# A masked dense layer and a LoRA layer on one core: the first loads cut in halves, fewer products with zeros, later loads of the first batch whole

## The chip, the cores and the metric

The kernel runs on one core of a Trainium2 chip. The metric is the time of one execution on the device in microseconds; lower is better. All data are fp32, and a mask is int32. Before the change the median of three runs is 395.52 us (395.45 to 395.57).

## The reference, cut to what matters

Eight batches of 256 tokens with 1024 features go through two linear layers, each with a residual. The first layer adds to its weight W0 a sign matrix, made from a mask of the batch's own and scaled by a coefficient of the batch. The second adds a product of rank 16 to a shared weight W1.

```python
# first layer: x is (8, 256, 1024), W (1024, 1024), mask (8, 1024, 1024)
output = einsum('bsi,oi->bso', x, W0) + b0
sign = 2 * mask - 1
x = x + output + einsum('bsi,bio->bso', x, sign) * coeff[:, None, None]
# second layer
base = einsum('bti,oi->bto', x, W1) + b1
lora = einsum('btr,bro->bto', einsum('bti,bir->btr', x, A[slot]), B[slot])
x = x + base + lora * 2.0
```

## The kernel before, in words

**One weight for each batch.** For batch b the kernel builds `coeff*(2*mask - 1) + W0 (+ identity, for the residual)` in SBUF and multiplies it with the batch's tokens. ScalarE turns the mask into the scaled sign (`convert`, L483 to L493, its records on L488); VectorE adds W0 (`add`, L385, records on L387); TensorE multiplies.

**Batch 0 is dense.** Its weight has 1024 input rows, cut into eight chunks c of 128 rows; a chunk has two parts i of 512 output columns. Loads of mask and W0 for each part (256 KB each, 2048 bytes to a partition) are issued on SP's queue in the order mask, W0, part after part (L522 to L531). The tokens of batch 0 come in between: chunk 0's on ACT's queue, chunk 1's on SP's (128 KB each), and those of two chunks at a time behind the first part of chunks 2, 4 and 6 (256 KB each). W0 stays in SBUF; later batches load masks only. For chunk 0, `parts` (L462) cuts the first part into two halves of 256 columns for converting, adding and multiplying, while the loads bring the part whole. The 64 matmuls of the dense batch (L570) run chunk after chunk, each 128x128 weights by 256 tokens. Each fp32 matmul shows as two passes in the records, so they are 128.

**Ahead of it** TensorE runs products with zeros (`idle`, L419, records on L422), which compute nothing that is used: columns 256 and 128 first, then one small product that spreads the coefficients over the partitions (L435), then 256, 256 and 128 columns (L441). From the coefficients VectorE makes `two_c` and `neg_c` (L445), which every convert needs.

**Batches 1 to 7** use products by quarter blocks with sums of weights and of tokens (`seven`, L718, seven products in place of eight; TensorE records on L761). Batch 1's masks go another way (L645). Masks come in blocks of 512 KB, 4096 bytes to a partition. **The second layer** works on four batches at a time with the same scheme twice over, and partly three times (`Deep`, records on L1144; plain leaves on L1089). Leaves of W1 that the second group of batches needs again are written to DRAM by the first group and loaded again (`left_again`, L919). Where a name is in `HALVES`, the saved innermost sums come as two loads of 128 KB in place of one of 256 KB (L943).

**The order of the work** is planned ahead of the run. `Plan.task` notes each piece of work with the time it should take; `plan.pe` is the time at which TensorE is expected to be free, from which due times come; `plan.order` (L153) then places all pieces on the five engines by a greedy rule, with a model of DMA rate and eight DMAs in flight, and picks the buffers. The instructions are issued in that order. First loads have a rank of their own (L517) and so keep the order in which they are written.

Of the kernel before, what the change touches and what calls it, by code (L numbers as in the profile page):

```python
# [9 lines left out]
I32 = mybir.dt.int32  # L10
# [3 lines left out]
P = 128  # L14
OH = 512
CG = 2
OQ = 256
# [6 lines left out]
A22_AT = 40.0  # L24
INNER_MOVED, INNER_AT = ({}, {o: ("t1", "t2", "t3", "t4") for o in ("S3", "A22")}), 24.0
SAVED = {(o, n) for o in ("A11", "S1", "S4") for n in ("a11", "s1")}
HALVES = ("A11",)
EARLIEST = 35.0
SHIFTED, MASKED = 5.2, 1.8
LEAF, SLACK = 30.0, 1.5  # L30
ALONE = 8.0
# [273 lines left out]
def kernel(  # L305
# [17 lines left out]
    NG, _, _, T = x0T.shape  # L323
    R = lora_b.shape[1]
    SLOTS = lora_b.shape[0]
    D = lora_b.shape[2]
# [12 lines left out]
    def fixed(name, shape, dtype=F32):  # L339
        return Buf(name, None, t=const.tile(shape, dtype, tag=name, name=name))  # L340
# [6 lines left out]
    w0_sb = fixed("w0", [P, NC, D])  # L347
# [11 lines left out]
    def big(name, a, b):  # L359
        return Buf(name, "B", (a, b))  # L360
# [4 lines left out]
    def small(name, a, b):  # L365
        return Buf(name, "S", (a, b))
# [12 lines left out]
    plan = Plan(2.9)  # L379
# [14 lines left out]
    def dma(engine, o, x, nbytes, due=None, ahead=None, slack=0.0):  # L394
        busy = {"SP": 0.37, "ACT": 0.36, "POOL": 0.53}[engine]
        reads = [x] if isinstance(x, Ref) else []
        writes = [o] if isinstance(o, Ref) else []

        def emit():
            ENGINE[engine].dma_start(  # L400
                o.ap() if isinstance(o, Ref) else o, x.ap() if isinstance(x, Ref) else x
            )

        return plan.task(
            engine, busy, plan.LATENCY[engine] + slack, emit, reads, writes, due, ahead, nbytes
        )

    def pe(n, busy, emit, reads, writes):
        return plan.task("PE", busy, 0.17, emit, reads, writes)
# [9 lines left out]
    def idle(*columns):  # L419
        def emit():  # L420
            for n in columns:
                nc.tensor.matmul(  # L422
                    idle_ps.t[:, 0, :n], lhsT=zeros[:, :P], rhs=zeros[:, :n], start=True, stop=True
                )

        pe(1, sum(columns) / 290, emit, (), (idle_ps((0,)),))
# [11 lines left out]
        (h_sb(h_rows), lb_pad((0, 1))),  # L438
        (c_ps((0,)),),
    )  # L440
    idle(T, T, T // 2)  # L441
    plan.pe = 5.2
    for o, f in ((two_c, 2.0), (neg_c, -1.0)):
        dve(
            lambda o=o, f=f: nc.vector.tensor_scalar_mul(o.t, c_ps.t[:, 0, :B], f),  # L445
# [6 lines left out]
    def x0_ref(p, c=None):  # L452
        return x0[p](ALL if c is None else (c,), (lambda t: t) if c is None else (lambda t: t[:, c]))
# [4 lines left out]
    def part(a, i):  # L458
        flat = a.rearrange("p i f -> (p i f)")
        return flat.rearrange("(i p f) -> i p f", i=2, p=P)[i]  # L460

    def parts(c):  # L462
        every = slice(0, OH)
        if c == 0:
            return [(0, slice(0, OQ)), (0, slice(OQ, OH)), (1, every)]
        return [(0, every), (1, every)]

    def halves(o):
        return tuple(q for q in range(2) if o.start < (q + 1) * OQ and o.stop > q * OQ)
# [36 lines left out]
    w_b0 = [big(f"w_0_{c}", 2, OH) for c in range(NC)]  # L506

    def w_part(c, i, o):
        return w_b0[c](tuple((i, q) for q in halves(o)), lambda t: t[:, i, o])

    def w0_part(c, i, o):
        return w0_sb(
            tuple((c, i, q) for q in halves(o)),
            lambda t: t[:, c, :].rearrange("p (h o) -> p h o", h=2)[:, i, o],
        )

    def first_loads(*load):  # L517
        k = dma(*load)
        k.rank = 1.0 + 0.001 * k.n

    every = slice(0, OH)
    for c in range(NC):  # L522
        for i in range(2):
            w = w_part(c, i, every)
            m = w.buf(w.keys, lambda t, f=w.index: f(t).bitcast(I32))
            first_loads("SP", m, part(mask[0, c], i), P * OH * 4)
            first_loads("SP", w0_part(c, i, every), part(w0T[c], i), P * OH * 4)
            if c < CG and i == 0:
                first_loads(("ACT", "SP")[c], x0_ref(0, c), part(x0T[0], c), P * T * 4)
            elif c % CG == 0 and i == 0:  # L530
                first_loads("SP", x0_ref(c // CG), x0T[c // CG], P * CG * T * 4)  # L531
# [19 lines left out]
    for c in range(NC):  # L551
        h, q = divmod(c * P, OH)
        for i, o in parts(c):
            w = w_part(c, i, o)
            m = w.buf(w.keys, lambda t, f=w.index: f(t).bitcast(I32))
            n = o.stop - o.start
            convert(w, m, 0, n)
            if c >= 1 and i == h and o.start <= q < o.stop:
                d = w_b0[c](((h, q // OQ),), lambda t, h=h, q=q: t[:, h, q : q + P])
                add(d, d, ident((0,)), P)  # L560
            add(w, w, w0_part(c, i, o), n)
    for c in range(NC):
        for i, o in parts(c):
            ots = [i * TPH + j for j in range(o.start // P, o.stop // P)]
            w = w_part(c, i, o)

            def emit(c=c, ots=ots):
                for ot in ots:
                    h, j = divmod(ot, TPH)
                    nc.tensor.matmul(  # L570
                        dense[ot // 2].t[:, ot % 2, :],
                        lhsT=w_b0[c].t[:, h, j * P : (j + 1) * P],
                        rhs=x0[c // CG].t[:, c % CG, :],
                        start=c == 0 and ot % 2 == 0,
                        stop=c == NC - 1,
                        skip_group_check=True,
                    )

            pe(
                len(ots),  # L580
                len(ots) * 0.4318,
                emit,
                (w, x0_ref(c // CG, c % CG)),
                [dense[d]((0,)) for d in sorted({ot // 2 for ot in ots})],
            )
# [277 lines left out]

    SOON = EARLIEST
    A_OF = {"a11": (0, 0), "a12": (0, 1), "a22": (1, 1)}
# [53 lines left out]
    def left_again(name, pairs=()):  # L919
# [21 lines left out]
        for n in saved:  # L941
            t = small(f"ls_{name}_{n}", 4, P)
            step = 2 if name in HALVES else 4  # L943
            for i in range(0, 4, step):
# [100 lines left out]
    def second_layer(group, before):  # L1045
# [35 lines left out]
        def product(ps, l, r, start=False, part=None):  # L1081
            parts = [(c, j) for c in range(CG) for j in range(2)]
            if part is not None:
                parts = parts[part : part + 1]

            def emit():
                lt, rt = l.ap(), r.ap()
                for c, j in parts:
                    nc.tensor.matmul(  # L1089
                        ps.t[:, j, :],  # L1090
                        lhsT=lt[:, c, j * P : (j + 1) * P],
                        rhs=rt[:, c, :],
                        start=start and c == 0 and j == 0,
                        stop=False,
                        skip_group_check=True,
                    )

            pe(len(parts), len(parts) * 0.4318, emit, (l, r), (ps((0,)),))
# [577 lines left out]
```

## Time and profile before

| | us |
|---|---|
| median of three runs | 395.52 |
| the profiled execution | 395.16 |
| its span, first to last instruction | 393.46 |
| first product with zeros starts | 0.90 |
| first matmul of the dense batch starts | 5.46 |
| first matmul of batch 1 starts | 34.54 |
| DMA: 102.50 MB, mean | 261 GB/s |

The span is what the profile shows of one execution; the execution's own time is longer by what lies around it. PE is TensorE's matmuls, PEld its weight loads, DVE VectorE, ACT ScalarE, POOL GpSimd, SP the engine that issues most DMAs. A row of the timeline gives start, duration, engine, line of the kernel, operation, output and inputs, how many instructions are merged in it, and in brackets how long the engine idled before and what ended that. A row of the chain gives start, duration and what ran. A row by stretches gives the stretch, its length, the busy time of each engine with its instructions, the granted TensorE clock, the DMA engines' share and GB/s.

### The profile page before, as it was taken

To read this page: it belongs to the slowest core of one execution; us is meant where nothing else is said; L and a number is where in the kernel's file an instruction comes from. 1 tells how busy PE (TensorE), PEld (TensorE's weight loads), DVE (VectorE), ACT (ScalarE), POOL (GpSimd) and SP (SyncE) were. 2 spreads that over 40 slices of the span, in tenths; PEclk is the share of its full clock that TensorE was granted. 3 is DMA by queue.
4 is the path that set the end of the run, shared out by engine and by line. 5 is a ranking of instruction groups with operands and counts; after the bars stand their busy time and mean duration, and the time that the engine had idled before them with its cause. 6 is when DMAs were issued, how large, how long until landed. Compare 5 with 4: busy or idle time off the path is not lost.

```text
span 393.5 us, 7725 instructions
## 1 busy us (share of the span) xinstructions
PE 389.7 (99%) x2920; PEld 363.8 (92%) x2920; DVE 352.2 (90%) x596; ACT 169.8 (43%) x314; POOL 84.2 (21%) x140
## 2 busy tenths in 40 slices
PE   9999999999999999999999999999999999999997
PEld 7889999999978898988899999999999789999896
DVE  3569999999897799989999989999996999999886
ACT  5469677516245221315615647373222563431210
POOL 1000202234734264252250330000000131241000
PEclk9999999999999999999999999999999999999999
DMA  8999999994899969989999998503702999995804
GB/s 290 389 389 410 404 300 389 318 346 156 198 269 290 270 239 368 417 247 317 348 347 338 291 260 304 191 1 108 242 0 61 262 238 265 324 255 101 263 31 185
DMA packets 39382, 102.50 MB, mean 261 GB/s; under 512 B 5170, under 2 KB 6322, under 8 KB 39346
## 3 DMA queue, kind: packets, MB, share of 16 engines
q1 hardware_dynamic: 27216, 68.76, 49.0%
q0 software_dynamic: 11840, 33.05, 32.5%
q8 instruction: 23, 0.38, 0.4%
q10 hardware_dynamic: 290, 0.20, 0.2%
q14 instruction: 13, 0.11, 0.1%
HBM read 65.82 MB, written 21.50 MB: 222 GB/s over the span
## 4 chain that ended last, share of the span: by engine, by line
PE 99%; DVE 0%; issue 0%
PE bank L761 44%; PE bank L1089 31%; PE bank L1144 11%; PE bank L570 7%; PE bank L1254 2%; PE bank L1223 2%; PE bank L422 1%; PE bank L1444 0%; PE bank L435 0%; DVE big L387 0%
## 5 line engine op out<-in xcount | busy, mean ns | idle before, releaser
L387 DVE TENSOR_TENSOR big<-big,big 128x1024 f32<-128x1024 f32 (+2 forms) x106 | 106.1, 1019 | 0.4 <-PE bank L761 0.4
L761 PE MATMUL bank<-small,big 128*128 128x128 f32 x896 | 104.6, 275 | 0.0
L761 PEld LDWEIGHTS bank<-small,big 128*128 128x128 f32 x896 | 102.3, 192 | 0.0
L387 DVE TENSOR_TENSOR big<-bank,big 128x512 f32<-128x512 f32 (+2 forms) x115 | 75.5, 678 | 15.0 <-PE bank L1089 8.2
L488 ACT ACTIVATE big<-big,neg_c,two_c 128x1024 f32<-128x1024 int32 (+2 forms) x65 | 71.1, 1123 | 19.4 <-DMA big<-mask 19.3
L761 PE MATMUL bank<-big,big 128*128 128x128 f32 x672 | 78.3, 275 | 0.0
L761 PEld LDWEIGHTS bank<-big,big 128*128 128x128 f32 x672 | 76.8, 192 | 0.1
L387 DVE TENSOR_TENSOR big<-big,w 128x1024 f32<-128x1024 f32 (+2 forms) x55 | 56.5, 1048 | 6.3 <-ACT big L488 3.4
L672 ACT ACTIVATE big<-bank,b 128x128 f32<-128x128 f32 x112 | 33.3, 367 | 52.7 <-PE bank L761 47.0
L391 ACT COPY bank<-bank 128x128 f32<-128x128 f32 (+1 forms) x42 | 14.4, 357 | 89.6 <-PE bank L1144 48.3
L1089 PE MATMUL bank<-small,small 128*128 128x256 f32 x168 | 40.2, 379 | 0.0
L1089 PEld LDWEIGHTS bank<-small,small 128*128 128x128 f32 x168 | 31.4, 190 | 3.9
L391 ACT COPY big<-bank 128x512 f32<-128x512 f32 x32 | 17.7, 594 | 36.0 <-PE bank L1254 17.4
L1089 PE MATMUL bank<-big,small 128*128 128x256 f32 x120 | 30.5, 381 | 0.0
L570 PE MATMUL bank<-small,big 128*128 128x256 f32 x128 | 29.2, 393 | 0.0
L570 PEld LDWEIGHTS bank<-small,big 128*128 128x128 f32 x128 | 25.4, 199 | 3.6
L477 POOL DMA_DIRECT2D big<-w x10 | 12.5, 1254 | 71.9 <-DMA big<-mask 56.5
L1089 PEld LDWEIGHTS bank<-big,small 128*128 128x128 f32 x120 | 21.4, 191 | 2.5 <-DVE big L387 0.4
L477 POOL DMA_DIRECT2D big<-big x14 | 12.3, 931 | 46.6 <-ACT big L991 36.1
L1089 PE MATMUL bank<-big,big 128*128 128x256 f32 x88 | 21.1, 383 | 0.0
L387 DVE TENSOR_TENSOR small<-big,small 128x512 f32<-128x512 f32 (+1 forms) x41 | 21.1, 522 | 0.0
L1089 PEld LDWEIGHTS bank<-big,big 128*128 128x128 f32 x88 | 16.5, 190 | 3.2 <-issue 0.4
(106 smaller groups left out, 468.6 us busy)
## 6 DMA issues: line engine op xcount, KB each, us to landing
big<-mask SPq DMA_DIRECT2D x56, 512.0 KB, 9.1
big<-xT SPq DMA_DIRECT2D x14, 512.0 KB, 8.6
big<-big POOLq DMA_DIRECT2D x14, 512.0 KB, 9.0
big<-w POOLq DMA_DIRECT2D x10, 512.0 KB, 10.3
big<-mask SPq DMA_DIRECT2D x16, 256.0 KB, 5.4
w<-w0T SPq DMA_DIRECT2D x16, 256.0 KB, 5.4
big<-w1T SPq DMA_DIRECT2D x8, 512.0 KB, 14.5
leaf_S_s<-small POOLq DMA_DIRECT2D x16, 256.0 KB, 7.6
```

The costliest lines, as they stand in the source:

```text
L387: return dve(lambda: f(o.ap(), x.ap(), y.ap()), n, (x, y), (o,), due, ahead)
L391: "ACT", n / 1200 + 0.06, 0.11, lambda: nc.scalar.copy(o.ap(), x.ap()), (x,), (o,), due
L422: nc.tensor.matmul(idle_ps.t[:, 0, :n], lhsT=zeros[:, :P], rhs=zeros[:, :n], start=True, stop=True)
L477: lambda: nc.gpsimd.dma_start(o.ap(), z.ap(), accum_op=ALU.add),
L488: lambda: nc.scalar.activation(o.ap(), x.ap(), AF.Identity, bias=neg_c.t[:, b : b + 1], scale=two_c.t[:, b : b + 1]),
L570: nc.tensor.matmul(dense[ot // 2].t[:, ot % 2, :], lhsT=w_b0[c].t[:, h, j * P : (j + 1) * P], rhs=x0[c // CG].t[:, c % CG, :], start=c == ...
L672: lambda o=o, p=p, bias=bias: nc.scalar.activation(o.ap(), p.ap(), AF.Identity, bias=bias.ap()),
L761: nc.tensor.matmul(ps[:, j, :], lhsT=l[:, c, j * P : (j + 1) * P], rhs=m[:, 2 * a + c, :], start=first and a == 0 and c == 0 and j == 0, s ...
L1089: nc.tensor.matmul(ps.t[:, j, :], lhsT=lt[:, c, j * P : (j + 1) * P], rhs=rt[:, c, :], start=start and c == 0 and j == 0, stop=False, skip ...
L1144: lambda: nc.tensor.matmul(o.ap(), lhsT=l.ap(), rhs=r.ap(), start=start, stop=False, skip_group_check=True),
L1223: nc.tensor.matmul(ph.t[i * S : i * S + R, 0, :], lhsT=la.t[:, i, c, :], rhs=y[GB * group + i, c // TPH].t[:, c % TPH, :], start=c == 0, s ...
L1254: nc.tensor.matmul(ps[b].t[:, j, :], lhsT=lb_pad.t[rows, o : o + P], rhs=h_sb.t[rows, :], start=j == 0, stop=j == 1, skip_group_check=True,)
```

## The change

- The second call of products with zeros has 256 and 128 columns, not 256, 256 and 128. `plan.pe` behind it is 4.75, not 5.2.
- Mask and W0 of chunk 0, first part, are loaded in two halves of 128 KB each. The second part, still loaded whole, is converted, added and multiplied in halves as well (`PARTS = 4`).
- Chunks 4 to 7 (`WIDE = 4`) load mask and W0 in one DMA of 512 KB each, mask first. The tokens that come in between follow behind both. Converting, adding and multiplying go on by parts. On the host these four chunks are no longer reordered by part, so that a partition's 4096 bytes are contiguous.
- `HALVES` is empty: the saved sums of A11 come whole.

```diff
-HALVES = ("A11",)
+HALVES = ()
+IDLE, FIRST = (256, 128), 4.75
+PARTS = 4
+WIDE = 4
...
-    idle(T, T, T // 2)
-    plan.pe = 5.2
+    idle(*IDLE)
+    plan.pe = FIRST
...
         if c == 0:
-            return [(0, slice(0, OQ)), (0, slice(OQ, OH)), (1, every)]
+            first = [slice(0, OQ), slice(OQ, OH)]
+            return [(0, o) for o in first] + [(1, o) for o in (first if PARTS == 4 else [every])]
...
+    def first_parts(c, i):
+        if c >= WIDE:
+            return ()
+        return (slice(0, OQ), slice(OQ, OH)) if c == i == 0 else (every,)
+
+    def wide(c):
+        m = w_b0[c](tuple((i, q) for i in range(2) for q in range(2)), lambda t: t.bitcast(I32))
+        first_loads("SP", m, mask[0, c], P * 2 * OH * 4)
+        o = w0_sb(
+            tuple((c, i, q) for i in range(2) for q in range(2)),
+            lambda t: t[:, c, :].rearrange("p (h o) -> p h o", h=2),
+        )
+        first_loads("SP", o, w0T[c], P * 2 * OH * 4)
+
     for c in range(NC):
         for i in range(2):
-            w = w_part(c, i, every)
-            m = w.buf(w.keys, lambda t, f=w.index: f(t).bitcast(I32))
-            first_loads("SP", m, part(mask[0, c], i), P * OH * 4)
-            first_loads("SP", w0_part(c, i, every), part(w0T[c], i), P * OH * 4)
+            if c >= WIDE and i == 0:
+                wide(c)
+            for o in first_parts(c, i):
+                n = P * (o.stop - o.start) * 4
+                wo = w_part(c, i, o)
+                m = wo.buf(wo.keys, lambda t, f=wo.index: f(t).bitcast(I32))
+                first_loads("SP", m, part(mask[0, c], i)[:, o], n)
+                first_loads("SP", w0_part(c, i, o), part(w0T[c], i)[:, o], n)
...
-    for k in range(D // P):
+    for k in range(WIDE):
         by_part(arrays["mask"][0, k])
         by_part(arrays["w0T"][k])
```

## The prediction

> **What bounds the kernel now.** I read the page first: the share of busy time and the chain that ended last.
>
> ```profile
> PE 389.7 (99%) x2920; PEld 363.8 (92%) x2920; DVE 352.2 (90%) x596; ACT 169.8 (43%) x314; POOL 84.2 (21%) x140
> PE 99%; DVE 0%; issue 0%
> ```
>
> TensorE is busy for 389.7 of 393.5 us and the chain is made of nothing else. The list of waits for TensorE alone has one row, and it is the start of the program:
>
> ```profile
> PE bank L422 <- PEq L1665: 0.9, 1, 0.9
> ```
>
> So from 0.90 us on nothing holds TensorE; time can only be gained by giving it fewer passes, a faster clock, or less idling. (Each fp32 matmul is two passes in the records.) Second, the chain in order of time:
>
> ```profile
> 0.90 1.62 PE bank L422 x4
> 2.52 0.72 PE bank L435 x2
> 3.24 2.43 PE bank L422 x6
> 5.67 29.03 PE bank L570 x128
> 34.70 71.46 PE bank L761 x640
> ```
>
> L422 are the products with zeros, L435 the coefficients, L570 the dense batch. The timeline of the first microseconds shows what the dense batch waits for:
>
> ```profile
> 3.17 2.50 PE L422 MATMUL bank<-const-float32-0.0 128*128 128x256 f32 x6
> 3.36 0.15 DVE L445 TENSOR_SCALAR neg_c<-bank 128x8 f32<-128x8 f32 x1
> 3.75 1.09 ACT L488 ACTIVATE big<-big,neg_c,two_c 128x256 f32<-128x256 int32 x2 [0.44 <-DMA big<-mask]
> 4.76 0.76 DVE L387 TENSOR_TENSOR big<-big,w 128x256 f32<-128x256 f32 x2 [1.24 <-DMA w<-w0T]
> 5.26 24.73 PEld L570 LDWEIGHTS bank<-small,big 128*128 128x128 f32 x108
> 5.46 1.06 PE L570 MATMUL bank<-small,big 128*128 128x256 f32 x2
> ```
>
> The first weight (5.26) comes just behind both the last zero product and the first add. Third, the speed of the passes, L570 alone in stretches of 3 us (the count in brackets is that of passes):
>
> ```profile
> 5.40:8.40 3.00, 2.94 (x7) 2.42 (x8) 1.00 1.06 392
> 8.40:11.40 3.00, 3.00 (x15) 2.64 (x14) 1.00 1.04 384
> ```
>
> 7 passes start in 3 us before 8.4, and 14 to 15 after. The single passes start 0.427 us apart until 8.4 and 0.216 us after it (13.82 to 34.54: 96 passes in 20.72 us). The clock column says 1.00 in both, since the granted clock has no record before 8.38 us; the doubling of the rate is what counts. So the dense batch begins at half speed, and an advance there is worth only half.
>
> **The change, part by part.**
>
> *Products with zeros.* The second call falls from 256+256+128 to 256+128 columns: two passes of 256 columns at 0.427 us, 0.85 us. TensorE is then free for the dense batch at 5.46 - 0.85 = 4.61.
>
> *First loads in halves.* Mask and W0 of chunk 0, first half, come as 128 KB each. Two loads of 256 KB issued in steady state (the SP rows at 14.34 to 17.72, five steps) land 0.676 us apart, so 128 KB are worth 0.34. The mask half lands at 3.75 - 0.34 = 3.41, but neg_c ends at 3.36 + 0.15 = 3.51; with the 0.09 us that such a start takes after its landing ScalarE starts at 3.60. Conversion 1.09/2 = 0.55, to 4.15. W0's half has 0.68 less ahead of it and lands at 4.0, so the conversion decides: add from 4.2, 0.76/2 = 0.38, to 4.58. Before, the weight load came 0.12 us behind the add's end (5.14 to 5.26) and the first matmul 0.20 behind that: 4.9. The x0 load on ACT's queue (128 KB) landed at 4.81; if it does not move, the first matmul comes at 4.81 + 0.05 + 0.20 = 5.06; if it moves by 0.68, it does not decide. I take 4.95, between the two, for TensorE: 0.51 us sooner, with some 0.34 us idle after the last zero product. Ends: 5.06 (0.40 sooner) and 4.61 (0.85, all the data on time).
>
> *Worth of it.* If full speed still comes at 8.4, 0.51 us hold 0.51/0.427 = 1.2 passes that are no longer done later at 0.216: 1.2 x 0.216 = **0.26 us**. Ends: 0.20 and, with no idle time, the two removed passes, 0.43.
>
> *The second half and the second part of chunk 0.* The second half's weight is wanted four cold passes on, at 6.66; before, it was ready at 5.52. Its loads now are issued at 1.77 and 2.24 in place of 0.86 and 1.30, but carry half; by the same 0.34 us steps it is ready some 0.1 us either side of 5.5. Part two is used in halves, loaded whole, and issued 0.94 later (two SP issues of 0.47). It was ready at 6.25 + 0.69 = 6.94; ScalarE takes 2 x 0.55 for 0.81, VectorE 2 x 0.38 for 0.69. Even with all of it, 6.94 + 0.94 + 0.36 = 8.24, and it is wanted at 4.95 + 8 x 0.427 = 8.37. Cost nothing; that cover is thin only at this worst end.
>
> *What the two extra issues do to later loads.* Between nothing (the DMA engines have a backlog and bytes decide) and 0.94. From 5.3 on the DMA share is above 1.0, so I take 0.2. Cover: chunk 1's first weight is ready at 7.97 + 0.69 = 8.66 and used at 10.37; 1.7 us, of which 0.26 + 0.2 go.
>
> *Whole loads, chunks 4 to 7.* Sixteen issues become eight. A part must now wait for all of W0: for chunk 4 the add starts no sooner than the last byte, which arrived near 18.41 + 0.68 = 19.09, less the x0 load (256 KB, 0.68) that now comes behind it, so 18.4, with the 0.2 18.6. Add 0.69: 19.3. Now it is 17.23 + 0.69 = 17.92, and TensorE wants it at 13.82 + 32 x 0.216 = 20.73, less 0.26: 20.47. Cover 1.2 us, 0.5 at the worst end. x0 of that group lands at 19.3 also. Chunk 7: its last W0 landed at 28.85; less the 0.6 below, plus 0.2, an add of 0.69 and an identity add of 0.29, its first part is ready at 29.4, wanted at 30.8. No cost. The masks behind gain: loads of 512 KB are issued 1.28 us apart (eight from 30.22 in 9.29 us), two of 256 KB take 1.35, so eight save 0.6 us, 0.4 net of the 0.2.
>
> *HALVES empty.* Two loads of 256 KB for four of 128 KB on SP (the rows at 243.68 to 249.22, deep_A). The last landing is near 252.4 and the first product that reads them starts at 298.18; nothing either way.
>
> **Does the gain reach the end?** It must pass the places where TensorE follows a load. After the dense batch two are close. The product with S1 of batch 1 starts after 96 passes of L761 from 34.54, 0.1117 us each: 45.26; its sum comes out of VectorE at 43.01 + 1.22 = 44.23. A later one starts at 64.91, behind these sums:
>
> ```profile
> 43.01 3.49 DVE L387 TENSOR_TENSOR big<-big,big 128x1024 f32<-128x1024 f32 x3
> 61.84 2.36 DVE L387 TENSOR_TENSOR big<-big,big 128x1024 f32<-128x1024 f32 x2
> ```
>
> 64.20 leaves 0.7. An advance of 0.26 goes through both, with the masks 0.4 sooner as well. Everything else close (as little as 0.12 us at 323.03) follows TensorE's own results, and moves with it.
>
> **Sum.** The profiled execution took 395.16, 1.70 more than its span of 393.46; 395.16 - 0.26 = 394.90. It lay 0.36 below the median of the runs, 395.52, so for the median I say **395.3**. Likeliest case's own range: 395.1 (0.43 gained) to 395.5.
>
> [...] The passes above doubled in rate 5.2 us after 3.17 and 7.5 us after 0.90. [...]
>
> **Rivals.**
>
> 1. *The cold stretch grows.* Zero products keep TensorE busy; taking them away opens a gap of 0.34 us at 4.61. If what brings full speed starts anew there, the stretch from 3.17 to 8.4 (5.2 us) counts from 4.95 and ends at 10.15: 1.75/0.427 = 4.1 passes, 0.211 us dearer each, +0.87, net +0.6: 396.1. If it is the stretch from 0.90 (7.5 us): 12.45, +2.0, net +1.7: 397.3. Middle 396.7; it costs more than 0.2% from a step at 10.6 us on. For: two gaps of 0.22 between weight loads, before 2.45 and 3.17, lie ahead of a late step. Against: those gaps did not keep it away, and the dense passes run on from 4.95. Chance 0.17, of which 0.03 within 0.2%.
>
> 2. *A new order brings waits.* The order of all work is planned from the start, and TensorE's due times move from 5.2 to 4.75; behind that any VectorE work may change places. If one 1024-column add (1.22) slips ahead of a link with 0.17 of slack (as at 334.46), TensorE stands 1.05: net +0.8, 396.3. That is where it decides. Against: not one wait in the order now. Chance 0.14, slower.
>
> 3. *Given back at a load.* If the masks of batches 1 and 2 come 0.7 late, the join at 64.91 takes all of it: 395.5. Against: the DMA figures above. Chance 0.09.
>
> 4. *Full speed sooner.* If the step is not tied to the start of the products, it may fall sooner; bound: all of 4.95 to 8.4 at full rate, 8.1 x 0.211 = 1.7, net -2.0; half of it 394.4. For it only that one profile shows one step. Chance 0.12.
>
> **How the numbers follow.** Forecast 0.48. A measurement of this kernel can tell about 0.2% (0.79 us) from no change: my gain is a third of that. Within: 0.48 + 0.09 + 0.03 = 0.60. Slower: 0.14 + 0.14 = 0.28. Faster: 0.12. The range for 8 in 10 runs from 394.8, which leaves most of rival 4 out, to 396.8, which holds rival 2 and the lower half of rival 1.
>
> **What would show it.** Four passes of L422 behind the coefficients, not six; the first L570 matmul at 4.9 to 5.1; L570 passes 0.427 apart until 8.4, and eight of them rather than seven; L761 beginning near 34.3; still no wait of TensorE behind 0.90 but the short one at 4.6. Wrong if the step of the rate moves, if TensorE has a wait of its own near 20, 45 or 65, or if L570 starts later than 5.2.

## The result, and the profile after

| | before | after |
|---|---|---|
| median of 22 runs each, taken in turn | 395.34 (394.62 to 396.08) | 395.89 (395.46 to 396.66) |
| ratio | | 1.0017, 95% interval 1.0011 to 1.0023 |
| span of the profiled execution | 393.46 | 393.91 |
| first matmul of the dense batch | 5.46 | 4.67 |
| first matmul of batch 1 | 34.54 | 34.94 |
| start of the last pass, less that of batch 1's first | 355.78 | 355.83 |

The kernel became slower by 0.55 us. That is inside the range of the forecast and inside 0.2%, but its sign is clear and is not the one forecast (395.3, a gain of 0.26). The last two rows say where to look: the dense batch begins 0.79 us sooner and ends 0.40 later, and what follows it takes as long as before. In 29 us the change loses 1.2 us.

The page after, its busy time and the chain:

```profile
PE 389.2 (99%) x2918; PEld 362.6 (92%) x2918; DVE 351.7 (89%) x597; ACT 169.9 (43%) x315; POOL 84.5 (21%) x140
PE 97%; DMA 1%; SPq 1%; DVE 0%; issue 0%; DVEq 0%
```

TensorE's work is that of before, less two passes. But the chain that was TensorE alone now runs through a DMA. The chain in order of time (start, length, what) shows where:

```profile
3.19 4.86 DMA w<-w0T
10.66 24.44 PE bank L593 x112
```

And TensorE's list of waits (total, times, longest) has a row that was not there before, ahead of the one at the start of the program (PEq, TensorE's sequencer):

```profile
PE bank L593 <- DVE big L390: 0.9, 1, 0.9
PE bank L425 <- PEq L1688: 0.9, 1, 0.9
```

(L593 is the dense batch, L390 the add, L492 the convert, L425 the zero products, L784 the seven products.) The timeline of the first microseconds after:

```profile
3.17 1.65 PE L425 MATMUL bank<-const-float32-0.0 128*128 128x256 f32 x4
3.55 0.60 ACT L492 ACTIVATE big<-big,neg_c,two_c 128x256 f32<-128x256 int32 x1 [0.26 <-DVE neg_c L448]
4.18 0.43 DVE L390 TENSOR_TENSOR big<-big,w 128x256 f32<-128x256 f32 x1 [0.67 <-ACT big L492]
4.67 3.06 PE L593 MATMUL bank<-small,big 128*128 128x256 f32 x8
7.42 1.09 ACT L492 ACTIVATE big<-big,neg_c,two_c 128x256 f32<-128x256 int32 x2 [2.29 <-DMA big<-mask]
8.17 0.80 DVE L390 TENSOR_TENSOR big<-big,w 128x256 f32<-128x256 f32 x2 [1.93 <-DMA w<-w0T]
8.65 1.56 PE L593 MATMUL bank<-small,big 128*128 128x256 f32 x6 [0.92 <-DVE big L390]
```

The first four rows are the change at its best: convert, add and first matmul each come 0.2 to 0.8 us sooner, and the zero products (by the pitch of the passes the last one ends at 4.61) meet the first weight nearly without a gap. The next three are the price. ScalarE idles 2.29 us for the mask of chunk 0's part two, which landed at 7.39 (before: 5.38); VectorE idles 1.93 us for its W0, at 8.05 (before: 6.09); TensorE stands. Its passes 7.35 and 8.65 lie 1.30 us apart in place of 0.216. The pace of the passes ahead of that does not matter: the weight was ready at 8.60 (8.17 + 0.43), and had full speed come at 8.4 as before, in place of 6.9, the first eight passes would still have been done by 8.3 (an estimate from 4.67 and the pitch of 0.427). How much the DMA engines moved from 0.9 to 8 us, one row of each kernel, before first (the last number is GB/s, the one ahead of it the DMA share):

```profile
0.90:8.00 7.10, 7.10 (x18) 5.60 (x19) 2.61 (x10) 4.20 (x6) 1.14 (x3) 1.00 0.89 304
```

```profile
0.90:8.00 7.10, 6.83 (x18) 5.04 (x18) 1.68 (x7) 3.26 (x6) 1.14 (x3) 1.00 0.76 236
```

68 GB/s over 7.1 us are 0.48 MB. At the steady rate of 390 GB/s that is 1.2 us of the whole stream of loads, not of part two alone. These are one execution of each kernel. The experiments below have six more profiles in which the first part is loaded whole; they moved 283 to 302 GB/s, mean of all seven 293, so the kernel before is the highest of its kind. Against the mean the lack is 57 GB/s, 0.40 MB or 1.0 us.

### The profile page after: what moved, and what is told of

Read it like the earlier page. It is cut to its first block, busy times and chain, and to the rows that moved or that the text cites. A ratio compares the mean times of both kernels' runs of the same rounds, so it can differ in the third digit from the quotient of the medians.

```text
span 393.9 us, 7714 instructions
## 1 busy us (share of the span) xinstructions
PE 389.2 (99%) x2918; PEld 362.6 (92%) x2918; DVE 351.7 (89%) x597; ACT 169.9 (43%) x315; POOL 84.5 (21%) x140
## 4 chain that ended last, share of the span: by engine, by line
PE 97%; DMA 1%; SPq 1%; DVE 0%; issue 0%; DVEq 0%
PE bank L784 44%; PE bank L1112 31%; PE bank L1167 11%; PE bank L593 7%; PE bank L1277 2%; PE bank L1246 2%; DMA w<-w0T 1%; SPq L403 1%; PE bank L1467 0%; DVE big L390 0%; DVEq L390 0%
## 5 line engine op out<-in xcount | busy, mean ns | idle before, releaser
L390 DVE TENSOR_TENSOR big<-big,big 128x1024 f32<-128x1024 f32 (+2 forms) x106 | 105.9, 1015 | 0.4 <-PE bank L784 0.4
L784 PE MATMUL bank<-small,big 128*128 128x128 f32 x896 | 104.7, 275 | 0.0
L784 PEld LDWEIGHTS bank<-small,big 128*128 128x128 f32 x896 | 102.3, 192 | 0.0
L390 DVE TENSOR_TENSOR big<-bank,big 128x512 f32<-128x512 f32 (+2 forms) x115 | 75.3, 676 | 14.5 <-PE bank L1112 8.2
L492 ACT ACTIVATE big<-big,neg_c,two_c 128x1024 f32<-128x1024 int32 (+2 forms) x66 | 71.2, 1110 | 22.7 <-DMA big<-mask 22.4
L784 PE MATMUL bank<-big,big 128*128 128x128 f32 x672 | 78.3, 275 | 0.0
L784 PEld LDWEIGHTS bank<-big,big 128*128 128x128 f32 x672 | 76.8, 192 | 0.1
L390 DVE TENSOR_TENSOR big<-big,w 128x1024 f32<-128x1024 f32 (+2 forms) x56 | 56.7, 1029 | 12.2 <-DMA w<-w0T 8.7
L593 PE MATMUL bank<-small,big 128*128 128x256 f32 x128 | 29.5, 391 | 0.9 <-DVE big L390 0.9
L593 PEld LDWEIGHTS bank<-small,big 128*128 128x128 f32 x128 | 24.9, 196 | 5.3 <-DVE big L390 1.7
L390 DVE TENSOR_TENSOR small<-big,small 128x512 f32<-128x512 f32 (+1 forms) x41 | 20.8, 516 | 0.0
```

The costliest lines, as they stand in the source:

```text
L390: return dve(lambda: f(o.ap(), x.ap(), y.ap()), n, (x, y), (o,), due, ahead)
L492: lambda: nc.scalar.activation(o.ap(), x.ap(), AF.Identity, bias=neg_c.t[:, b : b + 1], scale=two_c.t[:, b : b + 1]),
L593: nc.tensor.matmul(dense[ot // 2].t[:, ot % 2, :], lhsT=w_b0[c].t[:, h, j * P : (j + 1) * P], rhs=x0[c // CG].t[:, c % CG, :], start=c == ...
L784: nc.tensor.matmul(ps[:, j, :], lhsT=l[:, c, j * P : (j + 1) * P], rhs=m[:, 2 * a + c, :], start=first and a == 0 and c == 0 and j == 0, s ...
```

## The experiments

Theory A: the half loads leave the DMA engines short of work at the start, so everything behind them comes late. Theory B: the whole loads or the new order of the work cost the time. Theory C: fewer zero products keep TensorE at half speed for longer. Ratios are to the kernel before, with 95% intervals, five rounds of runs in turn for each kernel. Each kernel has one profile, of one of its executions.

### One suspect taken out, or one alone

**The changed kernel with the first part loaded whole** (`k1_whole`):

```diff
-        return (slice(0, OQ), slice(OQ, OH)) if c == i == 0 else (every,)
+        return (every,)
```

> The changed kernel with chunk 0's first part loaded whole again (one load of 256 KB for mask and for W0). Theory A (the half loads, 128 KB each and one issue of SP in 0.47 us, leave the DMA engines short of work between 2.5 and 6 us, so the second part of chunk 0 lands 2 us late): the mask of part two lands near 5.4 instead of 7.39, no stand of TensorE near 8, DMA share near 1 from 2.6 us on; the first dense matmul near 5.3, batch 1 starts 0.4 to 0.8 us sooner than in the changed kernel; ratio to before 0.9990 to 1.0005. Theory B (the whole loads of 512 KB or the new order of the work cost the time): still 1.0012 to 1.0022. Theory C (fewer zero products keep the slow clock on longer): as B.

Measured: 1.0019 (1.0007 to 1.0032), times from 394.73 to 397.14. Part two's mask lands at 5.68 and the DMA engines move 291 GB/s, both as theory A says; yet nothing is gained. The profile shows what took the place of the stand: the weights now come at 5.6, the zero products still end at 4.61, and in the open time TensorE idles:

```profile
5.62 2.93 PE L593 MATMUL bank<-small,big 128*128 128x256 f32 x6 [0.80 <-DVE big L390]
```

After that it runs at half speed for six more microseconds. Its L593 passes by stretches:

```profile
5.60:8.60 3.00, 2.98 (x7) 2.44 (x8) 1.00 1.06 365
8.60:11.60 3.00, 3.00 (x8) 2.37 (x8) 1.00 1.03 390
11.60:14.60 3.00, 3.00 (x14) 2.58 (x14) 1.00 1.06 397
```

Seven or eight passes in 3 us are the slow rate, 14 the fast one; the step is near 11.8. The profiled execution is the slowest of this kernel's twelve (397.14; median 395.78), so its step is a late one. In the others the loss must be smaller, and that it has the same cause there is not shown.

**The kernel before with the half loads alone** (`k2_halves`):

```diff
-HALVES = ()
+HALVES = ("A11",)
...
-IDLE, FIRST = (256, 128), 4.75
-PARTS = 4
-WIDE = 4
+IDLE, FIRST = (256, 256, 128), 5.2
+PARTS = 3
+WIDE = 8
```

> The kernel before with the half loads of chunk 0's first part alone; zero products, order constants, loads of 256 KB as before. Theory A: the mask of part two lands near 7.4 again and TensorE stands for part two of chunk 0; as the dense batch begins no sooner than 5.4, the stand is shorter by up to 0.8; ratio to before 1.0010 to 1.0025. Theories B and C: 0.9995 to 1.0005.

Measured: 1.0039 (1.0026 to 1.0052; five runs), more than theory A's 1.0010 to 1.0025. Theory A's stand is there, and longer than in the changed kernel, where a shorter one was expected:

```profile
7.85 0.81 ACT L492 ACTIVATE big<-big,neg_c,two_c 128x512 f32<-128x512 int32 x1 [2.87 <-DMA big<-mask]
8.70 0.69 DVE L390 TENSOR_TENSOR big<-big,w 128x512 f32<-128x512 f32 x1 [2.34 <-ACT big L492]
9.45 0.92 PE L593 MATMUL bank<-small,big 128*128 128x256 f32 x3 [1.29 <-DVE big L390]
```

Of the 1.44 us by which this profile's span is longer than that of the kernel before (394.91 and 393.46), 0.91 lie ahead of batch 1, which begins at 35.45. The other 0.53 come later, 0.36 of them behind the last pass; no run here says why.

**The changed kernel without the whole loads** (`k3_nowide`, `WIDE = 8`):

> The changed kernel with all of the dense batch's loads by parts (256 KB, only chunk 0's first part in halves). Theory A: the same stand near 8; the loads behind come up to 0.6 us later; ratio to before 1.0015 to 1.0035. Theory B: 0.9990 to 1.0005. Theory C: 1.0012 to 1.0022.

Measured: 1.0028 (1.0019 to 1.0037). Without the whole loads it is not better, so they are not the loss; the intervals of this and of the changed kernel overlap, so that they win back 0.1% is likely and not shown. The stand near 8 that theory A expected is not in this profile. Up to chunk 4 this kernel has the loads and the zero products of the changed one, yet here W0's first half landed at 4.74 in place of 3.94, and the first weight came late:

```profile
4.84 0.43 DVE L390 TENSOR_TENSOR big<-big,w 128x256 f32<-128x256 f32 x1 [1.33 <-DMA w<-w0T]
5.32 6.85 PE L593 MATMUL bank<-small,big 128*128 128x256 f32 x19 [0.51 <-DVE big L390]
```

Full speed came at 10.2, and by then part two (its mask landed at 6.89) was there. So the same start can cost a stand for part two in one execution and a gap ahead of the first weight in another.

**The kernel before with the shorter zero products and 4.75 alone** (`k4_idle`):

```diff
-    idle(T, T, T // 2)
-    plan.pe = 5.2
+    idle(T, T // 2)
+    plan.pe = 4.75
```

> The kernel before with the shorter second call of zero products and the earlier due time alone. Theory A: the first dense matmul comes near 5.25 as the add ends at 5.18, TensorE idles 0.6 us ahead of it; ratio 0.9990 to 1.0003. Theory C: the passes get fast later than before, ratio 1.0010 to 1.0045. Theory B, in the form of the new order alone: 1.0005 to 1.0020.

Measured: 1.0012 (1.0002 to 1.0022). The dense batch begins at 5.06, 0.4 us sooner than in the profile before, and the kernel is slower: TensorE idles ahead of the first weight (0.23 us by the row; 0.45 from the end of the last zero product by the pitch), and full speed comes at 9.4.

```profile
5.06 7.13 PE L570 MATMUL bank<-small,big 128*128 128x256 f32 x22 [0.23 <-DVE big L387]
```

The earlier due time also moves much of VectorE's order behind 300 us, but from batch 1 on this profile takes 355.9 us, hardly more than the 355.8 of before.

### The two-by-two table

**The changed kernel with the long zero products back** (`k9_zeros`: `IDLE, FIRST = (256, 256, 128), 5.2`):

> The changed kernel with the long second call of zero products (256, 256, 128 columns) and 5.2 back; half loads and whole loads stay. If the two costs are separate (late part two from the half loads, late full speed from fewer zero products), the dense batch begins near 5.46 without a gap, full speed comes as in the kernel before, and the late data remain: ratio 1.0015 to 1.0035, no better than the changed kernel. If the zero products alone are to blame: 0.9990 to 1.0005.

**The same with the first part loaded whole as well** (`k14_corner`):

> The changed kernel with both suspects taken out (first part loaded whole, zero products as long as before, 5.2); whole loads for chunks 4 to 7, part two in halves and HALVES empty stay. If the two suspects are all that costs: 0.9980 to 1.0002, as with the whole loads alone. If the new order, the halves of part two or the empty HALVES cost: 1.0008 or more.

All four corners keep the whole loads for chunks 4 to 7, part two in halves and the empty HALVES:

| | first part whole | first part in halves |
|---|---|---|
| long zero products | 1.0006 (0.9995 to 1.0017) | 1.0014 (1.0004 to 1.0023) |
| short zero products | 1.0019 (1.0007 to 1.0032) | 1.0017 (1.0011 to 1.0023) |

With neither suspect the kernel can't be told from the kernel before. Its 1.0006 lies between the two forecasts (up to 1.0002, and from 1.0008), and its interval reaches 1.0017, so that the halves of part two and the empty HALVES cost nothing is likely and not shown. Of the new order this corner says little. Compared record by record on VectorE, ScalarE, GpSimd and SP, the changed kernel's order departs from that of the kernel before in 29 places, the corner's, with 5.2 back, in only 9. What clears the order is the changed kernel's own profile, which has no wait of TensorE behind the dense batch and takes 355.83 us from batch 1 on, against 355.78.

Each suspect by itself is slower than before, and both together are no worse than one. The steps between the corners are within the intervals. The profiles suggest why they do not add up. In that of the changed kernel the half loads bring the first weight just as the short zero products end, so there is no gap and no longer slow stretch; what remains is late data. With whole loads the data are in time, and the gap opens. The kernel without the whole loads, above, shows that the half loads do not always come in time for this. In its execution the gap opened as well.

**The kernel before with the whole loads alone** (`k10_wide`: `WIDE = 4`, all else as before):

> The kernel before with nothing but the whole loads of 512 KB for chunks 4 to 7. Both theories: no stand in the dense batch, the masks of batch 1 land 0.4 to 0.6 us sooner, nothing gained as TensorE does not wait for them: 0.9990 to 1.0008. If the whole loads cost by themselves: 1.0010 or more.

Measured: 394.79 beside 395.08, 0.9991 (0.9982 to 1.0000). A gain of 0.3 us at the edge of what the runs can tell.

### Why half loads starve the DMA engines

**The halves as 64 partitions with rows of 2048 bytes** (`k8_rows`, on the run with the half loads alone):

```diff
-            for o in first_parts(c, i):
...
+            for n, o in enumerate(first_parts(c, i)):
+                rows = slice(64 * n, 64 * n + 64) if c == i == 0 else slice(0, P)
...
+                        at(keys, lambda t, f=f, rows=rows: f(t)[rows]),
+                        part(src, i)[rows],
```

> As the run with the half loads alone, but the halves are 64 partitions each with rows of 2048 bytes, so the same number of issues and bytes without short rows. Theory A (too few bytes issued): the mask of part two lands at 6.9 to 7.8 as with the halves by columns, ratio 1.0020 to 1.0050. If the rows of 1024 bytes are to blame: it lands at 5.4 to 5.9 and the ratio is 0.9995 to 1.0012.

Measured: 1.0056 (1.0043 to 1.0069); part two's mask lands at 7.92, 217 GB/s. Without the short rows the stream is no faster, so they are not all of the loss. The run does not clear them quite: these loads were issued 0.62 us apart in place of 0.47, and part two's mask at 3.37 in place of 2.71, so more of its delay is that of the issues. (A half weight here needs both loads, so the dense batch begins only at 6.44; the ratio holds that too.)

**W0's halves on ACT's queue, x0 on SP's.** A first version (`k7_queues`) also loaded the tokens of chunks 0 and 1 a second time, in another layout, so that its products are not the layer's, and the first dense product waited for them until 11.1 us. So its ratio of 1.022 says nothing of the theories.

> As the run with the half loads alone (which was 1.0039), but W0's two halves go on ACT's queue and x0 on SP's, so that five loads of 128 KB are issued by 2.2 us instead of 2.7. Theory A (too few bytes issued): the mask of part two lands near 5.7 to 6.5 instead of 7.8, the stand of TensorE at 7.8 shrinks from 1.4 to under 0.6, ratio 1.0005 to 1.0020. If the short rows or the split itself are to blame: the mask lands at 7 or later, ratio above 1.0025.

The same without that load (`k7b_queues`, on the run with the half loads alone):

```diff
-                first_loads("SP", w0_part(c, i, o), part(w0T[c], i)[:, o], n)
-            if c < CG and i == 0:
-                first_loads(("ACT", "SP")[c], x0_ref(0, c), part(x0T[0], c), P * T * 4)
-            elif c % CG == 0 and i == 0:
+                first_loads("ACT" if c == i == 0 else "SP", w0_part(c, i, o), part(w0T[c], i)[:, o], n)
+                if c == i == o.start == 0:
+                    first_loads("SP", x0_ref(0, c), part(x0T[0], c), P * T * 4)
+            if c == 1 and i == 0:
+                first_loads("SP", x0_ref(0, c), part(x0T[0], c), P * T * 4)
+            elif c and c % CG == 0 and i == 0:
```

> The run with the half loads alone (1.0039), with W0's two halves on ACT's queue and x0 on SP's, so that five loads of 128 KB are issued by 2.2 us instead of 2.7 (the earlier run of this edit also loaded x0 a second time, and says nothing). Theory A (too few bytes issued): the mask of part two lands at 5.7 to 6.9 instead of 7.8, the stand of TensorE for part two shrinks from 1.4 to under 0.6, ratio 1.0005 to 1.0025. If the small loads do harm however early they are issued: the mask lands at 7 or later, ratio above 1.0025.

Measured: 1.0023 (1.0014 to 1.0032). Part two's mask is issued at 2.24 and lands at 6.98, just later than foretold (6.9); the stand is 0.75 us (1.29 with the half loads alone), longer than the 0.6 foretold; 261 GB/s in place of 236. Two fifths of what was lost come back (1.0039 to 1.0023), as half of the delay in issuing does. Here the time of the issues was what was short (two more of 0.47 us ahead of part two's mask, one of them taken away), as the next run shows from the other side.

**Two loads of 32 bytes in SP's queue** (`k13_issues`, on the kernel before):

```diff
             first_loads("SP", m, part(mask[0, c], i), P * OH * 4)
+            if c == i == 0:
+                first_loads("SP", lb_pad(("d0",), lambda t: t[:1, 2 * P : 2 * P + B]), coeff, 32)
             first_loads("SP", w0_part(c, i, every), part(w0T[c], i), P * OH * 4)
+            if c == i == 0:
+                first_loads("SP", lb_pad(("d1",), lambda t: t[:1, 3 * P : 3 * P + B]), coeff, 32)
```

> The kernel before with two loads of 32 bytes on SP's queue, one behind the first mask and one behind the first W0, so that the second part's mask is issued at 2.7 us as with the half loads, while the loads that count stay whole. Theory A (too few bytes issued per issue): by 8 us the DMA engines have moved 1.7 MB or less in place of 2.0 to 2.1, the mask of part two lands at 6.6 or later, ratio 1.0010 to 1.0035. If loads of 128 KB are slow in themselves: the mask lands at 6.3 or sooner, ratio 0.9995 to 1.0012.

SP's queue of that run:

```profile
0.86 0.38 SPq L400 DMA_DIRECT2D big<-mask  x1
1.30 0.32 SPq L400 DMA_DIRECT2D lb<-coeff  x1
1.68 0.35 SPq L400 DMA_DIRECT2D w<-w0T  x1
2.07 0.28 SPq L400 DMA_DIRECT2D lb<-coeff  x1
2.40 0.33 SPq L400 DMA_DIRECT2D big<-mask  x1
```

Two loads of next to no bytes put the issue of part two's mask 0.63 us back (from 1.77 to 2.40). From 0.9 to 8 us the engines moved 257 GB/s, 1.82 MB. The seven profiles with whole loads have 283 to 304, mean 293: the lack against the mean is 0.26 MB, which is 0.65 us at 390 GB/s, and 0.47 to 0.86 us against the lowest and the highest of the seven. So the delay of the issue went into the stream in about its full size, as near as one profile can tell. The time of landing does not help: the mask landed at 6.51, but in the seven without the tiny loads it landed anywhere from 5.38 to 6.70. (With the half loads of the changed kernel and its relatives on SP's queue it was 6.89 to 7.92, later than in all seven.) The expectation of theory A was 1.7 MB and 6.6 us, with an issue at 2.7; the tiny issues were shorter than that. The ratio, 1.0010 (0.9998 to 1.0022), does not decide.

GB/s from 0.9 to 8 us in all of these:

| | GB/s |
|---|---|
| first part whole: before, corner, short zeros alone, changed with whole, much shorter zeros, 4-to-7 alone, narrow small product | 304, 302, 298, 291, 288, 285, 283 |
| two tiny loads added | 257 |
| W0's halves on ACT's queue | 261 |
| half loads: changed, alone, zeros back, by 64 partitions, no whole loads | 236, 236, 225, 217, 216 |

### What brings full speed

**Much shorter zero products** (`k6_gap`, the kernel before with `idle(T // 2)` in the second call):

> The kernel before, with 128 columns of zero products in the second call in place of 640, the due time left at 5.2: TensorE idles from some 3.8 us until the first weight at 5.2. Theory C: full speed comes no sooner than 8.6 in most executions and as late as 12, ratio 1.0015 to 1.0040, and a wide spread. If zero products do not matter to the clock: first dense matmul near 5.2, ratio 0.9990 to 1.0002.

Measured: 1.0062 (1.0049 to 1.0075). First weight at 5.2, TensorE idle for 1.2 us before it, full speed at 9.5. That is more than theory C's 1.0015 to 1.0040; its 8.6 and 12 for full speed were estimates of mine that rest on no run. The profiled execution, the slowest of five, has a second wait of 1.5 us ahead of 58.1; if the others have it, not all of 0.6% is the clock's.

**Zero products without a break** (`k5_bcast`): the coefficients are spread over the partitions by the DMA, and the small product is gone, with the breaks of TensorE around it (in the profile before, 0.22 us each between weight loads, ahead of 2.45 and 3.17).

```diff
-    dma("ACT", lb_pad((0,), lambda t: t[:1, :B]), coeff, 32)
+    dma("ACT", coef_sb((0,)), coeff[0].partition_broadcast(P), 4096)
...
-    idle(T, T // 2)
...
+    idle(T, T, T, T, T)
```

> The kernel before, with the coefficients spread over the partitions by the DMA itself in place of the small product, and zero products of 5 x 256 columns without a break from 0.9 to 5.3 us. [...] If the breaks do not matter: 0.9995 to 1.0005. Theory A says nothing of this run.

Measured: 1.0095 (1.0079 to 1.0112): a miss for another reason. (The profiled execution is the slowest of six: 400.41, median 398.53.) The coefficients landed at 5.37 (their one row before: 2.05) and the first mask at 5.21 (3.66), so TensorE stood 1.7 us. It shows two things all the same. Full speed came at 5.19, sooner than in any other profile of this case. And behind a wait of 1.9 us later on the granted clock was at half once more:

```profile
54.75 2.29 PE L750 MATMUL bank<-big,big 128*128 128x128 f32 x19
58.91 5.47 PE L750 MATMUL bank<-small,big 128*128 128x128 f32 x32 [1.88 <-ACT big L661]
64.22 1.95 PE L750 MATMUL bank<-big,big 128*128 128x128 f32 x16
```

The row by stretches for that place has the granted clock, 0.50, in its third place from the end:

```profile
59.80:63.20 3.40, 3.40 (x18) 3.40 (x17) 3.40 (x4) 1.17 (x3) 0.00 (x0) 0.50 1.05 381
```

**The small product over 128 rows** (`k11_full`: coefficients into row 0 of a block of zeros, `lhsT=h_sb.t[:, :P]`, x0 first on ACT's queue):

> The kernel before with the small product for the coefficients over all 128 rows (127 of them zero) instead of one, x0 ahead of the coefficients on ACT's queue, and 2 x 256 columns of zero products ahead of it, so that TensorE is busy without a break from 0.9 to the dense batch. [...] If the one-row product and its breaks do not matter: 0.9995 to 1.0005.

Measured: 1.0033 (1.0022 to 1.0043). The coefficients, issued 0.45 us later, landed at 3.98 behind the big loads and TensorE waited 1.2 us for them: the break that the edit was to close became longer. Full speed came at 7.6 for all that, sooner than in the profile before (8.4). It says nothing on the one-row product.

**The small product with 8 columns in place of 128, on the kernel with the whole loads alone** (`k12_narrow`):

```diff
-            c_ps.t[:, 0, :P], lhsT=h_sb.t[:1, :P], rhs=lb_pad.t[:1, :P], start=True, stop=True
+            c_ps.t[:, 0, :B], lhsT=h_sb.t[:1, :P], rhs=lb_pad.t[:1, :B], start=True, stop=True
```

The second call of zero products has 256, 256 and 256 columns.

> The kernel with nothing but the whole loads (0.9991), and the small product for the coefficients narrowed to 8 columns, with 3 x 256 columns of zero products behind it, so that TensorE's stretch of little work between 2.3 and 3.2 us is shorter. Theory C: full speed comes sooner in some executions, ratio 0.9960 to 0.9990, the lowest times under 394.3. If the stretch is not what keeps full speed away: 0.9985 to 0.9995.

Measured: 0.9992 (0.9984 to 1.0001), inside the forecast without theory C, and no better than the whole loads alone (0.9991). The lowest time, 394.20, is as theory C had it. The finer form of theory C, that the small product itself keeps full speed away, is not borne out.

The step to full speed in each profile, by the last gap ahead of it:

| TensorE without idle time from 3.2 us on until the step | step at us |
|---|---|
| before; changed; half loads alone; zeros back | 8.4; 6.9; 7.1; 6.1 |
| corner; whole loads alone; two tiny loads; two queues; narrow small product | 8.0; 9.1; 8.2; 6.4; 7.3 |

| idle for 0.23 to 1.19 us ahead of the first dense weight, which begins at | step at us |
|---|---|
| short zeros alone, 5.06; much shorter, 5.16; changed without whole loads, 5.32 | 9.4; 9.5; 10.2 |
| changed with first part whole, 5.62; halves by 64 partitions, 6.44 | 11.8; 9.4 |

The two groups do not overlap: 6.1 to 9.1, mean 7.5, and 9.4 to 11.8, mean 10.1. One profile each, so the means are rough, and the latest step of each group, 9.1 and 11.8, is from the slowest execution of its kernel. Three kernels fit neither row: the broadcast, without the small product (5.2); the small product over 128 rows, which idled 1.17 us ahead of that product and not of the dense batch (7.6); and the first version with two queues, which idled 5.4 us (16.2).

## Why the prediction went wrong, point by point

- **What bounds the kernel**: right. TensorE's work is fixed, and batch 1 to the end took 355.8 us in the kernel before, the changed one, the corner and the whole loads alone. All that moved is ahead of batch 1.
- **First loads in halves**: the price was good in the profiled execution, the forecast there even too careful. ScalarE started at 3.55 (forecast 3.60), the add at 4.18 (4.2); a half takes 0.60 and 0.43, a little longer than the 0.55 and 0.38 I took. The first matmul came at 4.67, not 4.95: behind a wait the weight load started 0.05 us after the add's end (4.66 and 4.61) and the matmul with it, where I took 0.12 and 0.20 from a place in which the weight load was queued behind zero products. So the gap of 0.34 us that I put in was not there, and the gain at the start was 0.79 us, not 0.51. That is in part luck: of the four kernels that have these half loads in columns on SP's queue, two had W0's first half at 3.76 and 3.94, and two at 4.64 and 4.74, too late for such a start. The second half's weight was ready at 6.04, not near 5.5; it was wanted at 6.53, so that cost nothing.
- **The step that failed: what the two extra issues do to later loads, "I take 0.2".** It measured 0.48 MB, 1.2 us of the stream, against the profile before, and 0.40 MB, 1.0 us, against the mean of seven profiles with whole loads. I read the DMA share above 1.0 from 5.3 us on as a backlog that would cover a later issue. In the time that matters, 2.5 to 6 us, the changed kernel has none (DMA share 0.80; before 1.04): SP issued one load in 0.47 us, and 128 KB are moved in 0.34 (half of the 0.676 between landings of 256 KB). In the run with two tiny loads the delay of an issue there went into the stream in about its full size (0.63 us in, 0.26 MB or 0.65 us out). The issues of part two are 0.94 us later, 0.37 MB; what is left to 0.40 or 0.48 lies within the spread of the seven whole-load profiles (2.01 to 2.16 MB).
- **Part two of chunk 0, "wanted at 8.37, ready at 8.24 even with all of it"**: ready at 8.60 and 8.97, wanted at 7.56. Both sides were off: landing 2.0 us later than before where I allowed 0.94, and the eight passes ahead of it done sooner, as they began at 4.67 and ran at full speed from 6.9. (The 2.0 is against 5.38, the earliest of seven whole-load landings; against their mean of 5.9 it is 1.5.) The sum fits: 8.65 + 120 passes x 0.216 = 34.57, and three short delays behind the stand (0.10, 0.18, 0.10) make 34.95; the profile has 34.94. The 0.18 is chunk 1's first weight, ready at 10.60 in place of 8.66: the cover of 1.7 us that I gave it was gone as well.
- **"If full speed still comes at 8.4"**: it does not come at a fixed time at all. In kernels with the long second call of zero products and no gap it came at 6.1 to 9.1. That spread is worth 3.0/0.427 x 0.211 = 1.5 us (an estimate), and single executions of the kernel before do differ by up to 1.5 us. That the step is the cause in each of them is not shown. Three of them within 0.12 us were luck. So 0.26 us was a sum over a step that one execution showed; half of each gained microsecond is right only where the slow stretch lasts beyond it.
- **Whole loads of chunks 4 to 7**: right. No stand behind chunk 1, and the stream behind gains; alone they are worth 0 to 0.18%.
- **HALVES**: no cost seen (the corner, within its interval). **Rival 2, a new order**: the order did change (29 places, see above), but no wait came of it: behind the dense batch TensorE has none, and that part takes 355.83 us against 355.78.
- **Rival 1, the longer slow stretch**: seen in other profiles, and not in that of the changed kernel, whose step came at 6.9. In these profiles it went with a gap behind the last zero product. Where one opened, the step came 2.5 us later on average, which would make 2.5/0.427 x 0.211 = 1.2 us (an estimate); the medians of the two in which nothing else was late (short zeros alone, changed with the first part whole) are only 0.38 and 0.54 us above the kernel before. How often such a gap opens in the changed kernel is not known.
- **Rival 3, given back at a load**: near. At 65.31 the slack was 0.11 us (the sum ended at 65.20; before, 0.7). In the runs with two tiny loads and with two queues batch 1 began at 34.44 and 34.60, and the rest then took 356.5 and 357.1 us, 0.7 and 1.3 us more than 355.8, as if a late stream were paid for behind the dense batch there.
- **Rival 4, full speed sooner**: it did come sooner, at 6.9 in place of 8.4, and gained nothing, as the passes then waited for part two until 8.65.

## What to carry to other kernels

At the start of a kernel count the bytes that each issue brings: here a smaller first load could give the first operand sooner (first matmul at 4.67 in place of 5.46) and put all that was issued behind it later by one issue of 0.47 us, and there was no backlog to hide that (DMA share 0.80 from 2.5 to 6 us). Two edits that each fill the hole which the other leaves have to be tried together and apart; here each alone is slower than before, and so is the pair. One profile shows one execution: the same loads landed up to 1.3 us apart from one profile to the next (5.38 to 6.70), so a landing time is to be compared with several. Before a gain of a fifth of a per cent is put down to anything, look at how far single executions of the same kernel lie apart.

## What the runs showed of the hardware that was not expected

- The step of TensorE from 0.427 to 0.216 us a pass came at no fixed time: at 5.2 to 16.2 us in the profiles, 2.9 to 6.2 us after the last gap ahead of it (or, where there was none, after the break around the small product, which ends at 3.17; in the run with the broadcast, after the start). In the run with the broadcast the granted clock was 1.00 from 40.00 to 59.70 us, 0.50 from 59.80 to 63.20 and 1.00 from 63.30 to 80.00. What sets these times is not shown.
- Full clock was lost after one idle time of 1.88 us (run with the broadcast, ahead of 58.91). Idle times of 1.74 us (same run, behind the step at 5.19), 1.51 (much shorter zero products, ahead of 58.13) and 1.29 (half loads alone) left it at full speed. Idle times of 0.23 to 1.19 us just ahead of the dense batch, before the step, went with a late one.
- A load of 32 bytes to each of 128 partitions took 4.5 us to land at the start of the program, and the first mask beside it landed 1.6 us later than before; one row of 32 bytes on the same queue took 1.2.
